# Mixture-of-experts tiles handled in pairs: one turn and one down product for two tiles, and a scheduling list that counts changes of the array's column mode

## The chip, the cores and the metric

One core of a Trainium2 chip (trn2) runs the whole program. The metric is device time in microseconds (us) of one execution, as the median of several runs; 3 runs of the kernel before are given. A separate execution was taken by the hardware profiler; all durations below come from that one.

## The reference

The input x is 8 sequences of 256 tokens, 128 wide (2048 tokens). Six residual steps follow each other, the first three on one set of weights and the last three on another:

```python
x = x + 0.5 * ffn0(layernorm(x))     # mixture of experts, 8 experts, top 2
x = x + attn0(layernorm(x))          # causal attention, 16 heads of 8, low-rank q/kv
x = x + 0.5 * ffn0(layernorm(x))     # the same mixture of experts again
x = x + 0.5 * ffn1(layernorm(x))     # token mix: sigmoid(r) * (relu(k)^2 @ W_v)
x = x + attn1(layernorm(x))          # nine gated, shifted copies of a value product
x = x + 0.5 * ffn1(layernorm(x))     # the token mix again
```

The change lies in `ffn0`, which runs twice. For each token it takes the two best of 8 experts and adds their outputs, weighted:

```python
gu = normed @ gate_up_weight[e].T            # 128 -> 704
gate, up = gu[..., :352], gu[..., 352:]
hidden = silu(gate) * up
out_e = hidden @ down_weight[e].T            # 352 -> 128
moe_out += combine[..., e] * out_e           # combine is 0 outside the top 2
```

Everything is computed in fp32 (the routing counts in bf16 and fp16, where the numbers are small whole ones).

## The kernel before, in words

The 2048 tokens lie in four groups (`NG`) of four tiles (`GT`) of 128 tokens each; x stays in SBUF. A mixture layer (`moe_layer`, `moe_route`, `moe_plan`, `moe_experts`, `moe_back`) first writes the normalised rows to DRAM and finds each token's two experts. `moe_plan` sorts the 4096 pairs of token and expert into 36 expert tiles (`TILES`) of 128 rows; each tile is two halves of 64 rows (`U`), and each half has one expert. The plan is made twice: first from the first two groups (12 full tiles), then from all four (the other 24), so that expert work can begin early. The place of each row is found on VectorE by comparisons (tiles named `hit`, `at`, `slot`, `past`, `until`) and by small matmuls (`pc`, `pp`, `pi`, `pe`) on TensorE; the row numbers land in `take`. GpSimd then gathers rows by indirect DMA (`xs<-rows,take`).

One expert tile passes through these operations, all recorded in `moe_tile` (names are those in the profile):

- `pg`, `pu`: the gate and the up product, 64 rows and 352 columns per half, so that each half fills 64 columns of TensorE's array. The first half's weights are read in place by an expert number in a register (`gu`), the second half's from a copy (`wg`) made by ScalarE or VectorE.
- `sg`: silu of `pg` on ScalarE. `hid`: `sg` times `pu` on VectorE, 128x352.
- `ph`: three transposes ("the turn") of `hid`, over all 128 columns of the array.
- `hT`: copy of `ph` from PSUM to SBUF, on ScalarE or VectorE.
- `po`: the down product, three steps for each half, again 64 columns per half, with weights in place (`dw`) and copied (`wd`).
- `ys`: copy to SBUF, then a store to DRAM, from where `moe_back` gathers each token's two rows (`back<-ys,slot`) and adds them to x.

So `pg`, `pu` and `po` use the array in strips of 64 columns, and `ph`, like `pt` (transposes of gathered or normalised rows), `pl`, `pi` and the warming matmuls `pw`, uses it whole. Attention's score products `sc` use 32 rows, its value products `po<-ep,va` 32 columns. An fp32 product shows twice its number of matmuls in the profile.

The order of all this is not written by hand. Every operation is recorded in a list with the engine it runs on (or a choice of ScalarE and VectorE, `either`), an estimated duration, what it needs and which buffers it takes and frees. `Work.issue` then walks the list as a simulation: it gives each operation a rank (the longest chain behind it, moved by `BIAS` for the groups of the later stages) and always emits the operation that can start first, with a preference for a higher rank within 0.3 us. The emitted order is each engine's program order, and the engines keep to it. Where the simulation sees TensorE idle for long, `keep_warm` emits filler matmuls (`pw`) in the gap. PSUM's eight banks are the buffers `b`; `hid` and `hT` have 2 buffers each, `wg` and `wd` 3 each, `ys` 4.

The kernel is one stream of stages that overlap where the list lets them: routing and the first mixture layer, attention, routing and the second mixture layer, then for each group a mix, a shift step (`FOLD` says how its nine products are summed: pairs are added on GpSimd, and each sum goes into PSUM through an identity product `po<-ident,q`), and a second mix. In the profile every instruction has line L70, because all engines are called through one recording helper.

## Time and profile before

| | us |
|---|---|
| runs | 511.12, 512.78, 512.19 |
| median | 512.19 |
| the profiled execution's own time | 510.68 |
| its span, first to last instruction | 508.5 |
| TensorE busy | 485.4 (95%) |
| VectorE busy | 351.0 (69%) |
| ScalarE busy | 293.4 (58%) |
| GpSimd busy | 224.9 (44%) |

The profile lists for each group of like instructions the engine, the operation, output and inputs, how many there were, how long all took, and what ended the idle time ahead of them. In the names of columns, PE is TensorE's matmuls, PEld its weight loads, DVE VectorE, ACT ScalarE, POOL GpSimd, SP the queue that issues most DMAs. "The chain" is the run of work that ended last, followed back from the end; in it each piece lasts until the next piece of the chain begins, so that the time an engine needs to change over from one kind of work to the next is counted to one of the two.

The granted TensorE clock has a mean of 0.98. The mixture layers, on the span's time axis: the first expert product starts at 32.1 us and the first layer's last down product ends at 150.8 us; attention's last value product ends at 294.9 us; the second layer's first product starts at 285.2 us, its second plan is found at 329.2 us, and its last down product ends at 415.6 us.

### The profile page before, as it was taken

To read this page: it belongs to the slowest core of one execution; us is meant where nothing else is said; L and a number is where in the kernel's file an instruction comes from. 1 tells how busy PE (TensorE), PEld (TensorE's weight loads), DVE (VectorE), ACT (ScalarE), POOL (GpSimd) and SP (SyncE) were. 2 spreads that over 40 slices of the span, in tenths; PEclk is the share of its full clock that TensorE was granted. 3 is DMA by queue.
4 is the path that set the end of the run, shared out by engine and by line. 5 is a ranking of instruction groups with operands and counts; after the bars stand their busy time and mean duration, and the time that the engine had idled before them with its cause. 6 is when DMAs were issued, how large, how long until landed. Compare 5 with 4: busy or idle time off the path is not lost.

```text
span 508.5 us, 13883 instructions
## 1 busy us (share of the span) xinstructions
PE 485.4 (95%) x5206; PEld 312.9 (62%) x5206; DVE 351.0 (69%) x1217; ACT 293.4 (58%) x580; POOL 224.9 (44%) x240
## 2 busy tenths in 40 slices
PE   7978999999999999999999999599999998999995
PEld 4535666565666775776767766365666665566673
DVE  8788566476757986668786366935677755979770
ACT  3346676676355455455557566166767556586542
POOL 7084872563006600000027000278766568786731
PEclk9899999999999999999999999689999999999998
DMA  8941212231001100000201101022222111000001
GB/s 269 305 130 49 68 49 57 58 68 44 12 23 38 51 1 3 3 22 4 64 13 51 26 1 43 16 75 67 42 76 53 48 48 42 1 1 1 23 21 41
DMA packets 25984, 25.53 MB, mean 50 GB/s; under 512 B 3872, under 2 KB 23328, under 8 KB 25504
## 3 DMA queue, kind: packets, MB, share of 16 engines
q1 hardware_dynamic: 20368, 15.21, 9.7%
q0 software_dynamic: 4352, 8.92, 7.4%
q8 instruction: 42, 0.69, 0.6%
q10 hardware_dynamic: 1200, 0.53, 0.4%
q14 instruction: 22, 0.18, 0.1%
HBM read 16.78 MB, written 8.91 MB: 51 GB/s over the span
## 4 chain that ended last, share of the span: by engine, by line
PE 74%; DVE 11%; POOL 4%; issue 3%; ACT 1%; DMA 0%; POOLq 0%; ACTq 0%; DVEq 0%
PE sc L70 18%; PE po L70 15%; PE pg L70 9%; PE pu L70 9%; PE ph L70 6%; PE pt L70 5%; PE pgt L70 2%; DVE at L70 2%; PE pv L70 2%; POOL q L70 2%; PE pr L70 2%; PE pj L70 2%; POOL back L70 2%; DVE x L70 1%; PE pk L70 1%
## 5 line engine op out<-in xcount | busy, mean ns | idle before, releaser
L70 POOL DMA_INDIRECT xs<-rows,take x72 | 70.2, 976 | 48.3 <-issue 15.7
L70 POOL DMA_INDIRECT back<-ys,slot x64 | 61.3, 957 | 60.3 <-issue 45.4
L70 ACT ACTIVATE ep<-sc 128x512 f32<-128x512 f32 x96 | 52.3, 595 | 50.4 <-PE sc L70 46.8
L70 POOL TENSOR_TENSOR stats<-stats,minus_half 128x4 f32<-128x4 f32 x28 | 29.0, 1034 | 103.3 <-DVE stats L70 102.5
L70 DVE TENSOR_TENSOR hid<-sg,pu 128x352 f32<-128x352 f32 x71 | 36.8, 518 | 37.5 <-PE pu L70 35.9
L70 PEld LDWEIGHTS po<-dw,hT 128*64 128x64 f32 x432 | 49.9, 138 | 19.7 <-issue 15.9
L70 PE MATMUL po<-dw,hT 128*64 x432 | 60.0, 277 | 0.9 <-ACT sg L70 0.3
L70 PE MATMUL po<-wd,hT 128*64 128x128 f32 x432 | 60.1, 277 | 0.0
L70 ACT COPY wg<-gu 128x704 f32 x61 | 47.4, 779 | 19.7 <-PE pu L70 9.8
L70 PE MATMUL pg<-gu,nT 128*64 x144 | 57.4, 480 | 0.6 <-ACT nT L70 0.5
L70 PEld LDWEIGHTS sc<-kT,qT 32*128 32x128 f32 x768 | 46.0, 186 | 19.3 <-issue 17.3
L70 PE MATMUL pg<-wg,nT 128*64 128x352 f32 x144 | 57.4, 480 | 0.0
L70 PE MATMUL sc<-qT,kT 32*128 32x128 f32 x768 | 56.7, 283 | 0.0
L70 PE MATMUL pu<-wg,nT 128*64 128x352 f32 x144 | 56.2, 472 | 0.0
L70 PE MATMUL pu<-gu,nT 128*64 x144 | 56.2, 472 | 0.0
L70 PE MATMUL sc<-kT,qT 32*128 32x128 f32 x768 | 55.2, 284 | 0.0
L70 DVE TENSOR_REDUCE mtmp<-sc 128x4 f32<-128x512 f32 x64 | 41.4, 684 | 14.2 <-PE sc L70 14.0
L70 PEld LDWEIGHTS po<-wd,hT 128*64 128x64 f32 x432 | 49.9, 138 | 0.0
L70 PEld LDWEIGHTS sc<-qT,kT 32*128 32x128 f32 x768 | 47.4, 186 | 3.3 <-issue 2.1
L70 ACT ACTIVATE sg<-pg 128x352 f32<-128x352 f32 x72 | 33.4, 463 | 27.6 <-PE pg L70 22.3
L70 ACT COPY hT<-ph 128x384 f32<-128x384 f32 x56 | 26.7, 479 | 29.1 <-PE ph L70 27.5
L70 PE MATMUL ph<-ident,hid 128*128 128x128 f32 x216 | 39.2, 293 | 1.5 <-DVE hid L70 1.1
(227 smaller groups left out, 1056.1 us busy)
## 6 DMA issues: line engine op xcount, KB each, us to landing
ys<-ys SPq DMA_DIRECT2D x72, 64.0 KB, 1.5
gu<-in_guT SPq DMA_DIRECT2D x2, 1408.0 KB
rest<-in_rest SPq DMA_DIRECT2D x1, 1280.0 KB
xs<-rows,take POOLq DMA_INDIRECT x72
x<-in_x SPq DMA_DIRECT2D x4, 256.0 KB
dw<-in_dwT SPq DMA_DIRECT2D x1, 1024.0 KB
rows<-rows SPq DMA_DIRECT2D x2, 512.0 KB
back<-ys,slot POOLq DMA_INDIRECT x64
```

The lines of the kernel that those rows point to most:

```text
L70: ins = do(*args, **kw)
```

## The change

Two expert tiles that follow each other are recorded as a pair. `moe_tile` becomes a generator that stops where the turn and the down product were, and the new `moe_pair` records one turn operation for both tiles (two banks, six transposes) and one down product operation for both (two banks, twelve products); the copies, the gating and the store stay as they were, one for each tile. No instruction of the computation itself is added or removed.

The list now knows two states of TensorE, strips or whole. `strips` is set on `pg`, `pu` and the pair's `po`. An operation on the other state than the one before starts `SWITCH` = 0.1 us later in the simulation, and is put behind by another `STICK` = 0.1 us when the next operation is chosen. The estimated durations of the weight copies change a little, `BIAS` (the ranks of the four groups' later stages, of the second layer's routing and of the first layer's second routing) has seven new numbers, and the last group's `FOLD` is made of pairs. A gate product waits in the list for the pair's turn before last (before: the tile's turn before last) and for the pair's down product before last (before: the third last tile's).

```diff
-BIAS = (27.0, 38.0, 18.0, 10.0, 25.0, 29.0, 1.0)
+BIAS = (32.0, 24.0, 8.0, 17.0, 27.0, 19.0, -1.0)
...
-FOLD = ((4, 4, 1), (2, 2, 2, 2, 1), (4, 4, 1), (4, 2, 1, 1, 1))
+FOLD = ((4, 4, 1), (2, 2, 2, 2, 1), (4, 4, 1), (2, 2, 2, 2, 1))
+TB, DB = 1, 1
...
+    SWITCH, STICK = 0.1, 0.1
+
     def start_on(self, op):
         t = self.free.get(op.engine, 0.0)
+        if op.engine == "pe" and op.us > 0.05 and op.strips != self.strips:
+            t += self.SWITCH
...
-            t, op = min(starts, key=lambda s: (s[0], -s[1].rank))
-            for t2, op2 in starts:
-                if op2.engine == op.engine and op2.rank > op.rank and t2 <= t + 0.3:
-                    t, op = t2, op2
+            starts = [
+                (t + self.STICK if op.engine == "pe" and op.strips != self.strips else t, t, op)
+                for t, op in starts
+            ]
+            at, t, op = min(starts, key=lambda s: (s[0], -s[2].rank))
+            for at2, t2, op2 in starts:
+                if op2.engine == op.engine and op2.rank > op.rank and at2 <= at + 0.3:
+                    at, t, op = at2, t2, op2
             ready.remove(op)
             if op.engine == "pe":
                 self.keep_warm(self.free["pe"], t)
+                if op.us > 0.05:
+                    self.strips = op.strips
...
                 for j in range(n):
-                    stored.append(
-                        moe_tile(r, plan, k0 + j, nT, nb, j, pus, turned, downs, numbers)
-                    )
+                    pair.append(moe_tile(r, plan, k0 + j, nT, nb, j, pus, turned, downs, numbers))
+                    if len(pair) == 2:
+                        stored += moe_pair(pair, turned, downs)
+                        pair = []
...
+    def moe_pair(pair, turned, downs):
+        ends = []
+        for tile in pair:
+            ends.append([next(tile)])
+        hids = [e[0][0] for e in ends]
+        banks = [Buf("b") for _ in pair]
+
+        def turn():
+            phs = []
+            for hid in hids:
+                phs.append(bank([P, len(HC), P], "ph"))
+                for c, c0 in enumerate(HC):
+                    nc.tensor.transpose(phs[-1][:, c, :], hid.out[:, c0 : c0 + P], ident)
+            return phs
+
+        ph = w.pe(0.68, turn, *hids, takes=banks, uses=[e[0][1] for e in ends])
+        turned.append(ph)
+        got = [tile.send((ph, n, banks[n])) for n, tile in enumerate(pair)]
+        out = [Buf("b") for _ in pair]
+        po = w.pe(
+            1.34, lambda: [down() for down, _, _ in got], *(n for g in got for n in g[1]),
+            takes=out, uses=[b for g in got for b in g[2]],
+        )
+        po.strips = True
+        downs.append(po)
+        return [tile.send((po, n, out[n])) for n, tile in enumerate(pair)]
...
         gates = w.either(
-            1.15, 1.05, lambda e: copied(e, "wg", gu, 2 * HID), plan["experts"], weights,
+            1.1, 0.9, lambda e: copied(e, "wg", gu, 2 * HID), plan["experts"], weights,
...
         backs = w.either(
-            0.85, 0.76, lambda e: copied(e, "wd", dw.rearrange("p e c d -> p e (c d)"), len(HC) * P),
+            0.84, 0.74, lambda e: copied(e, "wd", dw.rearrange("p e c d -> p e (c d)"), len(HC) * P),
...
-        pg = w.pe(0.6, lambda: product(0), known, nT, gates, weights, *pus[-1:], *turned[-2:-1], *downs[-3:-2],
+        pg = w.pe(0.6, lambda: product(0), known, nT, gates, weights, *pus[-1:], *turned[-1 - TB :][: len(turned) > TB], *downs[-1 - DB :][: len(downs) > DB],
                   takes=[bg], uses=[nb], spare=3)
         pu = w.pe(0.6, lambda: product(1), pg, takes=[bu], uses=[nb, gb])
         pus.append(pu)
+        pg.strips = pu.strips = True
...
-        ph = w.pe(0.34, turn, hid, takes=[bh], uses=[hb])
-        turned.append(ph)
+        ph, m, bh = yield hid, hb
...
-        po = w.pe(0.67, down, hT, backs, takes=[bo], uses=[tb, db])
-        downs.append(po)
+        po, m, bo = yield down, (hT, backs), (tb, db)
```

More of the change, by code (lines that the diff above doesn't have):

```diff
@@ L113, in __init__ @@
         self.out, self.end, self.rank, self.back = None, None, None, 0.0
+        self.strips = False
         self.choice = None
@@ L129, in __init__ @@
         self.buffers = {tag: [0.0] * n for tag, n in buffers.items()}
-        self.idle = None
+        self.idle, self.strips = None, False
     def op(self, engine, us, do=None, needs=(), takes=(), uses=(), lag=0.0, spare=0):
@@ L195, in keep_warm @@
         slots.append(a + n * us)
+        self.strips = False
         if self.idle is not None:
@@ L961, in moe_experts @@
     def moe_experts(r, sizes):
-        stored, numbers, pus, turned, downs = [], {}, [], [], []
+        stored, numbers, pus, turned, downs, pair = [], {}, [], [], [], []
         k0 = 0
@@ L1008, in moe_experts @@
                 for j in range(n):
-                    stored.append(
-                        moe_tile(r, plan, k0 + j, nT, nb, j, pus, turned, downs, numbers)
-                    )
+                    pair.append(moe_tile(r, plan, k0 + j, nT, nb, j, pus, turned, downs, numbers))
+                    if len(pair) == 2:
+                        stored += moe_pair(pair, turned, downs)
+                        pair = []
                 k0 += n
-        assert k0 == TILES
+        assert k0 == TILES and not pair
         return stored
     exps = {"left": 0, "all": 0}
+    def moe_pair(pair, turned, downs):
[22 more added lines that the diff above has]
+        return [tile.send((po, n, out[n])) for n, tile in enumerate(pair)]
     def moe_tile(r, plan, k, nT, nb, j, pus, turned, downs, numbers):
-        bg, bu, bh, bo = (Buf("b") for _ in range(4))
+        bg, bu = Buf("b"), Buf("b")
         sb, hb, tb, yb = Buf("sg"), Buf("hid"), Buf("hT"), Buf("ys")
@@ L1086, in moe_tile @@
         hid = w.dve(0.53, gated, sg, pu, takes=[hb], uses=[sb, bu, bg])
-        def turn():
-            ph = bank([P, len(HC), P], "ph")
-            for c, c0 in enumerate(HC):
-                nc.tensor.transpose(ph[:, c, :], hid.out[:, c0 : c0 + P], ident)
-            return ph
-        ph = w.pe(0.34, turn, hid, takes=[bh], uses=[hb])
-        turned.append(ph)
+        ph, m, bh = yield hid, hb
         def keep(engine):
             hT = wtile("hT", "hT", (P, len(HC), P))
-            copies(engine, hT, ph.out)
+            copies(engine, hT, ph.out[m])
             return hT
@@ L1116, in down @@
             return po
-        po = w.pe(0.67, down, hT, backs, takes=[bo], uses=[tb, db])
-        downs.append(po)
+        po, m, bo = yield down, (hT, backs), (tb, db)
         def result(engine):
             ys = wtile("ys", "ys", (P, P))
-            copies(engine, ys, po.out)
+            copies(engine, ys, po.out[m])
             return ys
         ys = w.either(0.3, 0.29, result, po, takes=[yb], uses=[bo])
-        return w.sp(
+        yield w.sp(
             0.45,
```

## The prediction

> **What bounds the kernel now.** I read the page's 40 slices first, then the chain that ended last, then the busy time by stage, then the chain again piece by piece inside a mixture layer.

> ```profile
> PE   7978999999999999999999999599999998999995
> ...
> PEclk9899999999999999999999999689999999999998
> ```
> ```profile
> PE 74%; DVE 11%; POOL 4%; issue 3%; ACT 1%; DMA 0%; POOLq 0%; ACTq 0%; DVEq 0%
> ```

> TensorE is the bound almost everywhere, and 74% of the chain is TensorE itself. One hole stands out, slice 26 (317 to 330 us), with a low clock in it and behind it. By stage (PE busy is the first number behind the length):

> ```profile
> 50.00:110.00 60.00, 60.00 (x566) 36.91 (x564) 35.52 (x111) 41.17 (x78) 36.93 (x36) 1.00 0.24 60
> ...
> 317.00:329.00 12.00, 6.41 (x50) 4.06 (x46) 11.59 (x52) 2.80 (x7) 1.63 (x2) 0.67 0.06 17
> 329.00:334.00 5.00, 4.80 (x20) 2.40 (x22) 1.20 (x9) 1.73 (x4) 3.66 (x4) 0.50 0.18 43
> ```

> In the first mixture layer (50 to 110 us) TensorE never stops, while DVE and ACT are busy for 36 and 41 of 60 us. What TensorE spends there beside products shows in the chain of 108 to 116 us (start, length, what):

> ```profile
> 110.13 0.59 PE pu L70 x4
> 110.72 0.97 PE pw L70 x4
> 111.69 0.33 PE ph L70 x3
> 112.02 0.74 PE pg L70 x4
> 112.76 0.59 PE pu L70 x4
> 113.36 0.66 PE po L70 x12
> 114.01 0.48 PE ph L70 x3
> 114.49 0.44 PE pt L70 x4
> 114.92 0.74 PE pg L70 x4
> ```

> A product behind a product takes 0.59 us, the same product behind a turn or transpose 0.74. A turn behind whole-array work (pw) takes 0.33, behind strips 0.48. So one change between strips and whole array costs 0.15 us, in each direction, and a turn alone among strips costs 0.33 + 0.30.

> [...] The row says 0.15. [...]

> **The change, stretch by stretch.** The built programs' PE order gives the counts. Over the whole kernel the changes of mode fall from 306 to 259, those at strips of 64 columns from 178 to 130. Matmuls are the same except fillers (101 to 94). My stretches are bounded by events in PE's order, their times are those of the trace.

> *First layer, first product to last down product (32.1 to 150.8 us).* 102 changes become 75: 27 x 0.15 = 4.05 us. TensorE is the bound, so it counts in full. The four fillers at 110.72 go as well: they stood where TensorE had no wait, 4 x 0.22 = 0.9 us. The eight fillers at 33.7 go too, but the gather they covered stays, so they give nothing. Sum -4.95.

> *Attention (150.8 to 294.9).* 119 changes in both. Fillers rise from 7 to 14, 1.5 us if they lie on the path, 0 if they fill a true wait; PE is busy 143.3 of 144 us there, so I take half: +0.8.

> *Attention's end to the second plan (294.9 to 329.2).* 24 changes become 19, but here TensorE waits: the plan runs on DVE.

> ```profile
> 321.18 2.50 DVE at L70 x8
> ...
> 328.62 0.43 DVE hid L70
> 329.19 0.87 PE ph L70 x3
> 330.07 1.37 PE pg L70 x4
> 331.44 0.83 PE ph L70 x3
> ```

> The saved 0.75 us only lengthens a wait. In the new DVE order two `hid` (0.52 each, +1.0) stand inside the plan's comparisons, where none stood. Ahead of the plan the transposes of the last group's rows (`pt`), its logits and its counts (`pc`) stand behind about as much expert work as before; adding up rows from attention's end I find the plan's first step about 1 us earlier (logits at 11.6 us behind it, against 12.5 now). Bounds -2 and +1; I take 0. The clock falls to 0.50 at 329 to 334 after this wait (pg 1.37 for 0.74), and I expect that again.

> *The rest of the second layer (329.2 to 415.6).* 60 changes become 45: -2.25. One product and one turn more lie ahead of the plan's wait and one down product fewer: -0.59 x 2 - 0.33 + 0.66 = -0.85. Against this, all 12 tiles of the first plan are now finished before the first transposes of the second, with five fillers about (+1.1), and the first product then waits for its rows' copy: 0.75 (DVE nT row) and 0.25 of hand-over less three fillers of 0.65, +0.35. Before, two down products (1.46 us in the chain) lay in that place. Sum -1.65.

> *Mixes and shifts (415.6 to the end).* The same 78.9 us of TensorE work, one filler more (+0.2). The new `BIAS` and `FOLD` change the groups' order, not the number of GpSimd adds (20, of 1.28 us). TensorE's waits here add up to 3.9 us, so at most about 3 can be won; one late add with its sum (1.28 + 0.89) bounds the loss at about 2. I take 0 for the order, as nothing in the trace decides it.

> *What the pairs put in place of the changes.* Copies, gating and stores stay. The rows:

> ```profile
> L70 DVE TENSOR_TENSOR hid<-sg,pu 128x352 f32<-128x352 f32 x71 | 36.8, 518 | 37.5 <-PE pu L70 35.9
> L70 ACT COPY hT<-ph 128x384 f32<-128x384 f32 x56 | 26.7, 479 | 29.1 <-PE ph L70 27.5
> ```

> The new steady order is turn of two, product pair (pg, pu), down of two, and between two such rounds one or two more product pairs. A `hid` begins 0.12 us behind its `pu` (94.83 to 94.95 in the trace) and takes 0.52; with 0.12 on to PE it is ready 0.76 us after `pu`. Between that `pu` and its transposes lie at least a product pair (1.18), the change (0.1) and the first tile's turn (0.33): 1.6 us. Both `hT`, even on one engine, end 0.33 + 0.12 + 2 x 0.48 = 1.4 us after the turn begins; the down product begins 0.75 + 1.23 = 2.0 us after it. The slack is 0.6 to 0.85 us each time, so the pair's own waits I put at 0. Their other bound is one DVE block in front (the four adds of a gather, 1.13 us): 0.3 us per pair. Weight copies move towards DVE (wg 11 to 27 at 0.54, wd 38 to 28 at 0.37: +4.9 us) and off ACT (wg 61 to 45 at 0.78, wd 34 to 44 at 0.51: -7.4 us); both have a third of their time free.

> *Sum.* -4.95 + 0.8 + 0 - 1.65 + 0.2 = -5.6 us. The profiled execution took 510.68 (span 508.5): 505.1. The median of the runs is 1.5 above that execution, so 506.5.

> **The rivals.** *More than that, about 502 (0.16).* For: the order's unknown, up to 3 us in the last stage, and the second plan's 4.1, 2.2 and 3.6 us of waits, in front of which more expert work now stands; if the longest falls away, so do parts of the 2.5 us lost at half clock. 506.5 - 3 - 1.5 = 502. Against: the plan's chain on DVE is as long as before.

> *The saving goes into waits, 512 (0.09).* The list had been too short by 0.15 per change, so TensorE ran later than planned and everything was ready early; with the changes gone it runs on plan and meets small delays of DVE and ACT. 0.18 us in each of the 30 pairs outside the plan's wait eats 5.5 us. For: the price now put in (0.1) is still under 0.15, so some lateness stays to hide delays, which speaks against this one.

> *Slower: the pair waits for its second half, 516 (0.13).* `hid` and `hT` have two buffers, and a pair holds both until its turn or down product has read them; the next pair's first `hid` then starts late, its PSUM banks stay taken (a pair takes up to four for products, two for turns, two for sums, of eight), and `pg` waits in PE's order with all behind it. [...] At 0.3 us on 30 pairs +9, so 515.6; it decides above 0.19 us a pair. Against: the slack above, and no fillers in the new order's first layer behind the first product.

> *It doesn't do what it says* is excluded by the counts: six transposes stand together in the built order.

> **How the numbers follow.** Forecast 506.5, chance 0.62, own range 503 to 510 (unknown order ±2.5, fillers ±0.8, plan -2 to +1). With the rivals, faster by over 0.3% (about what a measurement of this kernel can tell from no change, 1.5 us) is 0.78, within it 0.09, slower 0.13. The range runs from 501, inside the first rival, to 513, the end of the second.

> **What would show it.** In the new profile: turns of six matmuls at about 0.80 us in the chain with `pg` behind them at 0.74, once per pair; PE busy 100% from 50 to 110 us; the first layer from first product to last down product in about 113.5 us instead of 118.7; attention's end to second plan still 34 us, with a clock near half behind it; the second layer's rest about 1.7 us shorter. I am wrong if idle time before `ph` or `po` (now 1.5 and 0.9 us) grows to several us, if the plan's stretch grows, or if the last stage, 87 us from last down product to last matmul, moves by more than 2 us.

## The result, and the profile after

The kernel after takes 506.31 us (median of 4 runs, 505.23 to 508.04), the kernel before beside it 511.75 (median of 4, 511.12 to 512.78): ratio 0.989, 95% interval 0.987 to 0.991. Forecast was 506.5. The profiled execution took 506.38 (span 504.6), for 510.68 (508.5) before, so by the profiles the gain is 4.3 us, and by the medians 5.4.

The 40 slices and the chain by engine come first, as before:

```profile
PE   7979999999999999999999999799999999999995
...
PEclk9869999999999999999999799789999999999998
```
```profile
PE 77%; DVE 13%; issue 3%; POOL 2%; DMA 2%; ACT 1%; POOLq 0%; DVEq 0%
```

TensorE is still the bound, but the clock row has two new dents: slice 3 (25 to 38 us) is a 6 where it was a 9, and slice 23 (277 to 290 us, at attention's end) a 7 where it was a 9. The hole at the second plan is in the same place. By stretch (start and end, length, busy time of PE, PEld, DVE, ACT and POOL, granted clock):

```profile
50.00:110.00 60.00, 59.68 (x592) 39.45 (x591) 42.60 (x135) 39.30 (x83) 41.78 (x41) 1.00 0.25 64
283.20:290.00 6.80, 6.80 (x66) 4.59 (x64) 0.69 (x1) 2.56 (x6) 0.00 (x0) 0.50 0.01 2
317.00:326.00 9.00, 5.90 (x42) 4.21 (x40) 8.86 (x42) 1.88 (x4) 1.63 (x2) 0.71 0.01 3
326.00:331.00 5.00, 5.00 (x33) 3.33 (x32) 1.75 (x9) 1.91 (x4) 3.36 (x4) 0.50 0.16 45
```

The chain inside the first mixture layer, to be held against that of 108 to 116 us before:

```profile
105.68 0.81 PE ph L71 x6
106.48 0.74 PE pg L71 x4
107.22 0.59 PE pu L71 x4
107.82 1.31 PE po L71 x24
109.13 0.59 PE pg L71 x4
109.72 0.59 PE pu L71 x4
110.31 0.59 PE pg L71 x4
110.90 0.59 PE pu L71 x4
111.49 0.81 PE ph L71 x6
```

A turn of six takes 0.81 and slows the next `pg` to 0.74, once for two tiles; fillers are gone from this stretch. Waits of TensorE that bear on the pairs and the plan (in all, times, longest), after and then before:

```profile
PE pt L71 <- DMA xs<-rows,take: 2.2, 1, 2.2
PE pi L71 <- DVE at L71: 2.2, 2, 1.6
...
PE pe L71 <- DVE ef L71: 0.8, 1, 0.8
...
PE ph L71 <- DVE hid L71: 0.3, 1, 0.3
```
```profile
PE pi L70 <- DVE at L70: 4.8, 3, 4.0
...
PE ph L70 <- DVE hid L70: 1.1, 1, 1.1
```

Only 0.3 us is spent waiting for a `hid`, once in 36 pairs; before it was 1.1. `pi` waits for the plan's comparisons 2.2 us instead of 4.8.

I cut the span by TensorE events and split each stretch into the work itself, 0.15 us per change of mode, fillers, and what is left (waits, and half clock, which is a granted clock of 0.50). This table is worked out from the trace; the brackets hold the changes, the fillers in us and what is left in us, and the last column is the forecast.

| stretch | before | after | difference | forecast |
|---|---|---|---|---|
| up to the first product | 29.7 | 30.3 | +0.6 | 0 |
| first layer | 118.7 (102 changes, fillers 2.6, left 3.1) | 113.5 (75, 0, 4.5) | -5.2 | -4.95 |
| attention | 144.1 (119, 1.5, 8.3) | 146.3 (119, 3.0, 9.6) | +2.2 | +0.8 |
| to the second plan | 34.3 | 33.6 | -0.7 | 0 |
| rest of the second layer | 86.4 (60, 0, 4.3) | 84.1 (45, 1.1, 4.0) | -2.3 | -1.65 |
| mixes and shifts, to the start of the last group of products | 86.0 | 87.7 | +1.7 | +0.2 |
| sum | | | -3.7 | -5.6 |

The profiles' own times differ by 4.3; the other 0.6 is rounding and what lies outside the first and last matmul.

### The profile page after: what moved, and what is told of

Its sections match the earlier page's. It is cut to its first block, busy times and chain, and to the rows that moved or that the text cites. A ratio compares the mean times of both kernels' runs of the same rounds, so it can differ in the third digit from the quotient of the medians.

```text
span 504.6 us, 13830 instructions
## 1 busy us (share of the span) xinstructions
PE 485.7 (96%) x5199; PEld 317.9 (63%) x5199; DVE 355.0 (70%) x1207; ACT 285.0 (56%) x589; POOL 225.3 (45%) x240
## 4 chain that ended last, share of the span: by engine, by line
PE 77%; DVE 13%; issue 3%; POOL 2%; DMA 2%; ACT 1%; POOLq 0%; DVEq 0%
PE sc L71 17%; PE po L71 16%; PE pg L71 9%; PE pu L71 9%; PE ph L71 5%; PE pt L71 5%; PE pgt L71 3%; PE pr L71 3%; PE pk L71 2%; DVE st L71 2%; PE pv L71 2%; DVE stats L71 2%; PE pj L71 2%; POOL back L71 2%; DMA xs<-rows,take 1%
## 5 line engine op out<-in xcount | busy, mean ns | idle before, releaser
L71 POOL TENSOR_TENSOR stats<-stats,minus_half 128x4 f32<-128x4 f32 x28 | 29.1, 1038 | 105.0 <-DVE stats L71 104.2
L71 PE MATMUL sc<-qT,kT 32*128 32x128 f32 x768 | 57.9, 288 | 0.1
L71 PE MATMUL po<-dw,hT 128*64 x432 | 55.4, 279 | 0.0
L71 PE MATMUL po<-wd,hT 128*64 128x128 f32 x432 | 55.4, 279 | 0.0
L71 PEld LDWEIGHTS po<-dw,hT 128*64 128x64 f32 x432 | 48.6, 139 | 8.5 <-issue 6.4
L71 PEld LDWEIGHTS po<-wd,hT 128*64 128x64 f32 x432 | 48.7, 139 | 0.0
L71 ACT COPY wg<-gu 128x704 f32 x45 | 35.0, 779 | 13.8 <-PE pu L71 7.2
L71 PE MATMUL pgt<-yTg,rest 128*128 128x512 f32 x72 | 34.1, 600 | 1.1 <-DVE p L71 0.9
L71 PE MATMUL ph<-ident,hid 128*128 128x128 f32 x216 | 32.3, 285 | 0.3 <-DVE hid L71 0.3
```

The costliest lines, as they stand in the source:

```text
L71: ins = do(*args, **kw)
```

## The experiments

The first four ran on one chip, beside a kernel before of 511.25 us (median of 11, 510.09 to 512.52). Theory: the pairs save 0.15 us per change of mode they take away, and the list only follows. Rival: the list and the ranks, which order everything anew, are the gain or give it back. ("Ranks" are `BIAS`; old and new ones are always exchanged together with the `FOLD` of the last group in the first four kernels.)

**Pairs alone.** The kernel after with the old ranks and `FOLD`, the old estimates of the weight copies and no price on a change:

```diff
-BIAS = (32.0, 24.0, 8.0, 17.0, 27.0, 19.0, -1.0)
+BIAS = (27.0, 38.0, 18.0, 10.0, 25.0, 29.0, 1.0)
-FOLD = ((4, 4, 1), (2, 2, 2, 2, 1), (4, 4, 1), (2, 2, 2, 2, 1))
+FOLD = ((4, 4, 1), (2, 2, 2, 2, 1), (4, 4, 1), (4, 2, 1, 1, 1))
-    SWITCH, STICK = 0.1, 0.1
+    SWITCH, STICK = 0.0, 0.0
```

> Pairs alone: the kernel after, with the old BIAS, FOLD and copy estimates, and with SWITCH and STICK at 0. Its TensorE order has 256 changes of mode (before 306, after 259) and 101 fillers, as before. Theory (each change costs 0.15 us of TensorE where TensorE is the bound, and the pairs alone take the changes away): 50 x 0.15 = 7.5 us less, of which 0.75 in the plan's wait gives nothing; 505 us, within 503 to 508. Rival (the gain comes from the new list, its prices and ranks; pairs by themselves put as much into waits as they save): 511 to 515 us.

Measured 507.56 (505.53 to 508.84), ratio 0.992 (0.990 to 0.995). The pairs by themselves give 3.7 us, with 256 changes for 306: half of the 7.5 us that 50 changes at 0.15 come to. The first layer takes 114.9 us with 82 changes, for 118.7 with 102: 20 changes are worth 3.0 and its twelve fillers, which are gone, 2.6, against half clock from 33.8 to 37.2 us. From the second plan to the end this kernel takes 2.8 us more than the kernel before (175.2 for 172.4), though changes are fewer there too: what the pairs save can be lost in the order.

**List alone.** Single tiles as before, with `strips` set on `pg`, `pu` and `po` and the price in the list:

```diff
+    SWITCH, STICK = 0.1, 0.1
...
+        if op.engine == "pe" and op.us > 0.05 and op.strips != self.strips:
+            t += self.SWITCH
...
+        po.strips = True
```

> The list's prices alone: the kernel before, single tiles, old BIAS and FOLD, but with SWITCH and STICK at 0.1 and strips set on pg, pu and po. Its order has 317 changes of mode (11 more than before) and 128 fillers (27 more, 5.8 us). Theory: no change is avoided by pricing it, so 511.75 + 11 x 0.15 = 513.4 us, and up to 519 if the fillers lie on the path. Rival (the new list brings the gain): 506 to 509 us.

Measured 515.01 (513.83 to 515.54), ratio 1.007 (1.005 to 1.009). With single tiles the list does not avoid the changes (317 for 306). From attention's end to the last down product it needs 125.6 us where the kernel before needs 120.7. The 24 fillers in that stretch (5.2 us; before has none) are not the loss: they stand ahead of the second plan, where it needs 33.1 us for 34.3. Behind the plan it needs 92.5 for 86.4. There it has ten changes more, a product pair and a down product that stood earlier in the kernel before, and eight matmuls of the mixes (`pgt`); the mixes themselves get only 0.4 us shorter.

**Old ranks.** The kernel after with `BIAS` and `FOLD` of the kernel before (first four lines of the first diff), price and pairs kept:

> The kernel after with the old BIAS and FOLD; pairs and prices stay. 264 changes of mode, 96 fillers. Theory: the ranks only move the last stage and the attention's end; TensorE's order sums to 1.2 us more than after's, so 507.5 us, within 505.5 to 510. Rival (the ranks bring the gain): 510 us or more.

Measured 501.8 (499.62 to 503.77), ratio 0.981 (0.978 to 0.984). I missed this by 5.7 us and in sign: the new ranks and `FOLD` together cost 4.5 us, and without them the change gives 9.5. The stretches that shrink are attention (142.8 for 146.3) and mixes with shifts together with the rest of the second layer (169.9 for 171.8). Against that its first product starts 2.5 us later in this profile (32.8 us behind the first matmul for 30.3; 30.2 and 30.5 in two profiles of the same ranks with fillers, below). Attention agrees in the kernels without a price: 142.4 us with the old ranks (pairs alone), 146.3 with the new ones (next kernel). How the rest divides between ranks and `FOLD` was not tested.

**No price.** The kernel after with only the price gone (last two lines of the first diff):

> The kernel after with SWITCH and STICK at 0; pairs, new BIAS and FOLD stay. 254 changes of mode, 135 fillers (41 more than after, 8.8 us), 20 of them in the last stage and 18 in the wait for the second plan. Theory: the changes are as few, so only the fillers and what they stand for count; the 18 in the plan's wait are free or even help the clock, the others cost up to 5 us: 506 to 512 us. Rival (pricing the change is what avoids it): changes would have to rise, and they do not; it expects 512 or more.

Measured 518.12 (514.13 to 519.59), ratio 1.013 (1.010 to 1.016): a clear miss, and slower than before, with the fewest changes of all (254). Two thirds are lost where no strips exist at all, in mixes and shifts: 95.1 us for 87.7. There it has 8.8 us of fillers for 4.5, and TensorE waits for late partners. Waits of this kernel from 419 us on, then those of the kernel after from 410:

```profile
PE pt L71 <- ACT y L71: 1.7, 1, 1.7
PE po L71 <- POOL q L71: 1.7, 2, 1.3
```
```profile
PE pgt L71 <- DVE p L71: 0.9, 1, 0.9
PE pt L71 <- ACT y L71: 0.7, 1, 0.7
```

Together these give a table (medians, us; for pairs with old ranks and no price the copy estimates are the old ones too; 506.31 was measured beside a kernel before of 511.75, the others beside 511.25):

| | no price in the list | price in the list |
|---|---|---|
| single tiles, old ranks | 511.25 | 515.01 |
| pairs, old ranks | 507.56 | 501.8 |
| pairs, new ranks | 518.12 | 506.31 |

The price is worth 5.8 to 11.8 us with pairs and costs 3.8 without. With pairs it does not work by fewer changes: with old ranks there are 264 with it and 256 without. What falls is what is left over in the stretches (rest of the second layer 2.5 us for 5.1, mixes and shifts 4.7 for 6.5): my reading, argued and not tested by itself, is that the simulated times fit the real ones better, so that fewer engines meet late.

**What one change costs.** From here on all runs fell on two other chips (the last one on the second of them), where the kernel before takes 591 to 594 us and single stretches are disturbed (last section). Totals there are told, but mechanisms I read only in stretches without a disturbance. First, a small product between the two tiles' transposes, on 64 columns or on 128:

```diff
                 phs.append(bank([P, len(HC), P], "ph"))
+                if len(phs) == 2:
+                    nc.tensor.matmul(
+                        phs[1][0:64, 0, 0:8], lhsT=hids[0].out[:, 0:64], rhs=ident[:, 0:8],
+                        start=True, stop=True,
+                    )
```

The other kernel has 128 in place of both 64.

> The kernel after with one small product put between the two tiles' transposes in every turn: 128 rows deep, 64 columns of the array, 8 columns wide, so that TensorE goes from whole array to strips and back once more in each of the 36 pairs (72 more changes); its result is overwritten by the second tile's transposes. Nothing else differs, TensorE's order included. Theory (a change costs 0.15 us of TensorE's time): 72 x 0.15 = 10.8 us and the product itself (estimated 0.05 to 0.1 us, 2 to 4 us in all), less what the three or four pairs near the second plan lose in waits that are there anyway: 517 to 520 us, and 8.5 to 10.8 us above the kernel with the same product over the whole array. [...]

> The control: the same small product in the same place of each turn, over the whole array (128 columns), so that no change of mode is added. Both theories: the 36 products alone, 0.05 to 0.1 us each, so 508 to 510 us; the slot it takes in the turn is read from the chain.

Measured 586.55 (582.93 to 591.18) and 585.06 (574.07 to 588.9): the totals spread too far to tell. The turns do tell it. The chain of the kernel with the strip, then of the one without:

```profile
100.31 1.17 PE ph L71 x8
```
```profile
97.76 0.98 PE ph L71 x8
```

In nanoseconds the 21 turns that follow `pu` or `po` and precede `pg` take 1168 and 982 (medians), and 805 in the kernel after. Two changes cost 186 ns here, so 36 pairs would pay 6.7 us, less than my 8.5 to 10.8. The small product itself, which I had put at 0.05 to 0.1 us without a row for it, makes the turn of the control 177 ns longer (982 for 805).

The starts of the single matmuls show what a change is made of. In an ordinary turn of the kernel after they lie at 0, 164, 273, 382, 491 and 601 ns, and `pg` starts at 803. Inside the turn the starts are 109 apart. Going in, the turn starts 390 behind the last start of `pu`, where a product would start 289 behind it: 101 more; and its first matmul takes 55 more. Going out, `pg` starts 202 behind the last transpose, 93 more; and the pair of matmuls that opens it takes 347 where it takes 296 behind a product, 51 more. So a change is about 0.1 us in which nothing starts and 0.05 us by which the first matmul in the new state is longer, 156 ns in one direction and 144 in the other.

The small product shows both parts on its first change and little on its second. Between the two kernels the start ahead of it moves by 93, and its own first matmul by 49: 142, the full price. The change back adds only 21 and 22, since without a change, too, the next transposes follow the small product late (112 behind its last matmul, and 144 apart where they are 109 apart elsewhere). 186 is thus a price and a third, not two prices; why the small product hides the second was not tested.

**The attention ranks.** Attention's two ranks back, the rest of the kernel after kept:

```diff
-BIAS = (32.0, 24.0, 8.0, 17.0, 27.0, 19.0, -1.0)
+BIAS = (32.0, 24.0, 8.0, 17.0, 25.0, 29.0, -1.0)
```

> The kernel after with two of the seven ranks taken back: those that decide the second layer's routing and the first layer's second routing are again 25 and 29 (in the kernel after 27 and 19). 258 changes of mode and 90 fillers, against 259 and 94. Theory (the new ranks put sparse score products and little else at the end of attention, which lets the clock fall to half for 6.8 us there and costs about 3 us): no half clock at attention's end, attention about 143 us as in the kernel with all old ranks, total 502 to 504.5 us. Rival (what the old ranks gain lies in the last stage, whose five other new numbers stay): 505.5 to 507.5 us, attention still 146 us.

Measured 580.26 beside a before of 593.53, ratio 0.986 (0.980 to 0.993). A second run:

> The kernel after with two of the seven ranks taken back (second layer's routing 25 for 27, first layer's second routing 29 for 19), on a chip where the kernel before takes about 511 us. Theory (the new ranks leave sparse score products and little else at the end of attention, the clock falls to half for 6.8 us there and some 3 us are lost): no half clock at attention's end, attention about 143 us for 146.3, total 502 to 504.5 us. Rival (what the old ranks gain lies in the last stage, whose five other new numbers stay): 505.5 to 507.5 us, attention still 146 us.

583.9 beside 592.62, ratio 0.987 (0.981 to 0.992). Attention takes 172.8 and 174.7 us in these two. Four profiles of the same chip have the new ranks in attention: 178.9 and 175.9 (the next kernel), 174.8 and 171.3 (the two with the small product). The means are 173.8 and 175.2, and disturbances of about 30 us lie in each, so neither stretch nor total decides between theory and rival. Half clock that begins 9 to 12 us ahead of attention's last value product is in four of six profiles with the new routing ranks, and in none of eight with the old. That fits the theory that the ranks bring it; what it costs is not shown by these runs.

**Fillers in the first gather's wait.**

```diff
         pt = bank([P, GT, P], "pt")
+        for _ in range(warm):
+            nc.tensor.matmul(
+                pt, lhsT=ones_b, rhs=before.unsqueeze(1).to_broadcast([P, GT, P]), start=True,
+                stop=True,
+            )
...
+                warm = 9 if r["n"] == 0 and k0 == 0 else 0
```

> The kernel after with nine more fillers ahead of the first gathered rows' transposes, where TensorE otherwise waits 2.3 us for the gather. Theory (this wait starts the half clock that is in force from 30.7 to 37.5 us, and under which the first expert products lose 1.85 us): clock 1.00 there, the first products at 0.74 instead of 1.37, 504 to 505 us. Rival (the gather, or the clock state that the routing before it leaves behind, sets the time): 506 to 508 us, half clock still there or moved by a few us.

> The kernel after with nine more fillers ahead of the first gathered rows' transposes, where TensorE otherwise waits 2.2 us for the gather. Theory (this wait starts the half clock that is in force from 30.7 to 37.5 us, under which the first expert products lose 1.85 us): clock 1.00 there, first products at 0.74 instead of 1.37, 504 to 505 us. Rival (the gather, or the state that the routing before it leaves behind, sets the time): 506 to 508 us, half clock still there or moved by a few us.

Measured 581.53 (ratio 0.988, 0.980 to 0.996) and 582.4 (ratio 0.985, 0.981 to 0.989). The stretch itself lies ahead of the disturbances. First the kernel after, then the one with fillers (second run), both in windows that hold the wait and the first products:

```profile
30.70:37.50 6.80, 6.04 (x18) 1.91 (x18) 3.43 (x13) 2.43 (x5) 4.07 (x5) 0.50 0.12 36
```
```profile
30.70:37.50 6.80, 6.00 (x34) 1.91 (x31) 4.70 (x18) 4.14 (x10) 3.94 (x4) 1.00 0.26 81
```

and their chains, first after:

```profile
24.66 6.76 DMA xs<-rows,take
...
32.79 1.37 PE pg L71 x4
34.16 0.41 PE pt L71
34.57 1.37 PE pu L71 x4
35.94 1.17 PE pg L71 x4
37.11 0.56 PE pt L71 x2
37.67 0.74 PE pu L71 x4
```
```profile
24.64 7.27 DMA xs<-rows,take
...
32.74 0.81 PE pg L71 x4
33.55 0.26 PE pt L71
33.81 0.74 PE pu L71 x4
34.55 0.63 PE pg L71 x4
35.18 0.37 PE pt L71 x2
35.55 0.74 PE pu L71 x4
```

The same `pu` starts 2.1 us earlier, though the gather landed 0.5 later. The theory holds for this place: the wait was paid twice, and nine fillers in it take the second payment away. Half clock between 30 and 40 us is in all eight profiles of kernels with pairs and no fillers in this wait (3.4 or 6.8 us long), and in none of the four with them. What it does to the total is not shown. The kernel before had a wait of 1.9 us in the same place and kept its clock.

**Old ranks with fillers in both waits.** The kernel of 501.8 us, the nine fillers, and in the second plan's wait 8 ahead of the first `pi`, 2 ahead of each `pi` from the third on, and 10 ahead of `pe` (`fill3` sends so many fillers to the bank named):

```diff
+            if warm:
+                fill3(v["pb"], 8 if k == 0 else 0)
+                if k > 1:
+                    fill3(bank([P, GT, P], "pf"), 2)
...
+            if whole and r["n"] == 1:
+                fill3(pb, 10)
```

> Pairs and counting list with all ranks and FOLD of the kernel before (501.8 us in an earlier run), and fillers in two waits of TensorE that are followed by half clock: nine ahead of the first gathered rows' transposes, and in the second plan's wait eight ahead of the first place product (pi), ten ahead of the experts' product (pe) and two ahead of each later place product. Theory (these waits cost twice, once as a wait and once as half clock behind it): clock near 1.00 from 320 to 335 us, about 2.5 us less there and 1 us at the start, so 498 to 499.5 us. Rival (fillers take TensorE's time where it would have started earlier, and the clock falls anyway): 501 to 503 us.

> Once more the kernel with pairs, the counting list, all ranks and FOLD of the kernel before, and fillers in the wait for the first gathered rows (nine) and in the second plan's wait (eight, ten, and two ahead of each later place product), for its total on a chip where the kernel before takes about 511 us. Theory (both waits cost a second time, as half clock on the products behind them; without the fillers this kernel took 501.8): 498 to 499.5 us, with 0.74 for the first pg and clock 1.00 behind the second plan. Rival (the fillers only put work on TensorE's path): 501 to 503 us. Where the kernel before takes about 593, theory and rival both give 580 to 585, and only the clock behind the plan and the length of the stretches around the two waits tell them apart.

Measured 582.89 (ratio 0.987, 0.981 to 0.992) and 581.29 beside 591.35 (ratio 0.982, 0.978 to 0.985), on two chips where the kernel before takes over 590 us, so whether it beats 501.8 on the first stays open. Behind the plan it can be read. The old ranks without fillers, then with (second run), the 5 us behind the plan:

```profile
324.20:329.20 5.00, 5.00 (x41) 3.88 (x42) 2.47 (x11) 2.36 (x5) 3.35 (x4) 0.74 0.14 43
```
```profile
375.20:380.20 5.00, 5.00 (x65) 3.67 (x63) 3.94 (x23) 1.56 (x3) 1.05 (x2) 1.00 0.02 5
```

The down product behind the plan takes 1.36 us for 2.61, and since the fillers delay the last `pi` by 0.28, the next `pg` starts 0.97 us earlier, counted from attention's end. I had expected 2.5; half clock covered only part of the stretch in the kernel without fillers (0.74 in the window above, for 1.00).

## Why the prediction was right, and where its steps were off

**The price of a change and the first layer.** Forecast -4.95, measured -5.2. Its terms: 27 changes are 4.05 us, as forecast. I let the eight fillers at 33.7 us give nothing. All twelve were worth 2.6, not 0.9, and half clock from 30.7 to 37.5 us took 1.85 back on the first products, which I had not forecast: the right sum from one missing gain and one missing loss, which is luck. The run with nine fillers shows that loss. The 0.15 per change that I read from the rows stands, as about 0.10 ahead plus 0.05 in the first matmul (101 and 55 ns in one direction, 93 and 51 in the other).

**The pair's own waits.** Forecast 0, with 0.3 us per pair as the other bound: `ph` waits for `hid` 0.3 us in all. The rival of the late second half (516) did not come about.

**The second plan and the rest of that layer.** Forecast 0 and -1.65, measured -0.7 and -2.3. The waits for the plan's comparisons are shorter (2.2 us in all for 4.8, the longest 1.6 for 4.0), and half clock follows them as forecast (2.46 us lost).

**Attention.** Forecast +0.8, measured +2.2: the term of the sum that was mis-sized. Fillers count in full (+1.5; I took half), and the half clock at 283 to 290 us, which came with the new order and which I did not forecast, slows sixteen scores to 2.01 us for 1.09 and 32 value products to 1.87 for 1.04. With the old ranks the same place keeps its clock and gets through 106 matmuls for 66:

```profile
281.50:288.30 6.80, 6.80 (x106) 5.17 (x96) 0.95 (x4) 5.02 (x11) 0.00 (x0) 1.00 0.01 2
```

That difference is in part what half clock does, not why it comes. Just ahead of it the kernel after sends 38 matmuls in 3.2 us; but the kernel with old ranks, a little earlier, sends 38 in 4.0 and keeps its clock. First after, then old ranks:

```profile
280.00:283.20 3.20, 3.20 (x38) 2.61 (x37) 1.11 (x13) 2.08 (x4) 0.00 (x0) 1.00 0.00 0
```
```profile
274.30:278.30 4.00, 3.94 (x38) 2.77 (x38) 1.45 (x11) 3.85 (x8) 1.89 (x2) 1.00 0.42 115
```

PE counts as busy throughout or nearly so in both. Neither busy time nor the number of matmuls tells here whether the clock holds; the cause stays open.

**Mixes and shifts.** Forecast +0.2 with ±2.5 unknown, measured +1.7, inside that bound. I put the order at 0. The runs show two large terms in it: with pairs and old ranks the list's price gives 5.8 us, and the new ranks with their `FOLD` cost 4.5. That they nearly cancel is luck; nothing in the forecast said so.

**The total.** By the profiled executions I forecast -5.6 and -4.3 came. The medians moved by 5.4 because the execution profiled before lay 1.1 us under the median beside it, and the one after on its median. The 1.5 us that I added for the median did not come, and made up for the 1.3 that the stretches missed: the hit to 0.2 us is in part that luck. The mechanism was right where it was worked out: in the first layer the changes are gone and their time with them. But of the whole 5.4 us, pairs by themselves gave 3.7, and the rest comes, by the table above, from the order.

## What to carry to other kernels

Count changes of the array's mode on a stretch where TensorE never waits, read the price from the same product in both surroundings, and multiply: here 27 changes at 0.15 us carried a stretch forecast at 4.95 us that gave 5.2. When a change also renumbers priorities, the order it makes is a term of its own that may be as large as the gain (here -5.8 to -11.8 for the list's price, +4.5 for the ranks with `FOLD`): test it by itself, since the number of changes did not show it here. Removing fillers need not be a pure gain: in the first layer the twelve that went gave 2.6 us, and half clock from 30.7 to 37.5 us took 1.85 back; with nine fillers in the first gather's wait the clock there was 1.00.

## What the runs showed of the hardware

In all profiles half clock lasts 3.41 us or two, three or four times that (6.83, 10.24, 13.65), but for the piece that the end of the profile cuts: in the kernel before 3.41 and 13.65, in the kernel after 6.83 three times and 10.24. One of the 6.83 came at attention's end (clock 0.50 from 283.2 to 290 us), while PE counted as busy for all of 276 to 290 us.

On the two other chips the first layer, the rest of the second and attention grew by 19 to 33 us each, while the stretch to the second plan (33.5 to 34.4 us) and mostly the last stage did not. There VectorE and ScalarE stop for 3 to 10 us, again and again, while GpSimd sends a run of gathers. The timeline of the kernel with nine fillers (first run):

```profile
181.10 0.95 POOL L71 DMA_INDIRECT back<-ys,slot  x1 [0.30 <-DMA back<-ys,slot]
...
182.36 0.95 POOL L71 DMA_INDIRECT back<-ys,slot  x1 [0.31 <-issue]
183.61 0.95 POOL L71 DMA_INDIRECT back<-ys,slot  x1 [0.30 <-issue]
186.19 0.69 DVE L71 TENSOR_REDUCE mtmp<-sc 128x4 f32<-128x512 f32 x1 [9.48 <-remote]
186.25 1.09 ACT L71 ACTIVATE ep<-sc 128x512 f32<-128x512 f32 x2 [7.38 <-remote]
```

VectorE had stood for 9.5 us and ScalarE for 7.4 when they went on, 1.6 us behind the last of these gathers. In this profile 14 of VectorE's 17 stops of over 3 us behind the first 40 us have gathers in them; in the kernel after, on the first chip, none of three has, with gathers of the same length (0.97 us in the mean). What the cause is, no run here tells.
